# Where the outer sums of a nested Strassen-Winograd product are made: additions inside DMA transfers, another order of the outer products, and one addend taken with the PSUM read

## The chip, the cores and the metric

The kernel runs on one NeuronCore of a Trainium2 chip. The metric is device microseconds for one execution, as a median over runs. Five units matter here: TensorE (PE in the profile, with PEld for its weight loads), VectorE (DVE), ScalarE (ACT), GpSimd (POOL) and SyncE (SP), which here only issues DMA transfers. Each of them works through its own queue of instructions strictly in order; an instruction whose semaphore has not come holds everything behind it on that engine.

## The reference

What is computed, for x of 1024 x 512, 64 weight matrices (weight is 64 x 512 x 512, index e first), a linear weight of 512 x 512 and a bias, all in fp32:

```python
out_lin = x @ lin_w.T + lin_b
xv = jnp.einsum('bf,efm->bem', x, weight)
zp = jnp.einsum('bf,efm->bem', jnp.square(x), jnp.square(weight))
interaction = 0.5 * jnp.sum(jnp.square(xv) - zp, axis=1)
return out_lin + interaction
```

The second einsum needs no large product: the sum over e can be taken over the squared weight first, so it is one more product of 1024 x 512 by 512 x 512. The first one, x times a weight of 512 x 32768, is the work. Only the square of each element of xv is used, summed over e; the sign of a column of xv does not matter.

## The kernel before

**Tiling.** The 32768 columns (m and e together) are cut into 16 groups of 2048 columns. In a group the product (1024 x 512) by (512 x 2048) is done by Strassen-Winograd twice, one inside the other. The outer level cuts the group's weight into four quadrants w11, w12, w21, w22, each 256 x 1024 and 1 MB, held as two halves of 128 partitions x 1024 (`w11.0`, `w11.1` and so on), and replaces eight products by seven, numbered 1 to 7, of an x combination (`X1` to `X7`, made once at the start) with a weight combination. Products 1, 2, 3 use w11, w21, w22 as loaded; 5, 6, 7 and 4 use the outer sums T1 = w12 - w11, T2 = w22 - T1, T3 = w22 - w12 (written over w12) and T4 = w21 - T2 (written over w21; the sign that this form needs is in the x side). The order of the outer products is `ORDER = (1, 6, 2, 7, 4, 5, 3)`.

The inner level (`tree`, L393) does the same with each outer product: four sums t1 to t4 of 128 x 512 pieces of the weight combination, always on POOL, and then seven inner products, two matmuls of 128x128 by 128x512 each. That makes 7 x 7 x 2 = 98 matmuls a group and 1568 in all; 32 more for the linear part at the start and 32 for the squared weight at the end make 1632. An fp32 matmul is two PE records.

**From PSUM to the result.** The inner products go to three kinds of PSUM bank pair: b1, b3 and a ring of two b2. P5 goes to b3 first and is copied to an SBUF buffer p5 by ACT, then P3 is added in the same bank and the sum is copied to p53. P1 goes to b1 and is copied by ACT into the b2 pair that P6, P7 and P4 will add to. Each tree ends in four result positions (pos 0 to 3): for pos 0 and 2 DVE adds the PSUM bank to an addend in SBUF (`outer_psum`, L428), for pos 1 and 3 DVE adds p53 or p5 to the bank and a second addition of two SBUF buffers brings in the addend (`outer_sbuf`, L442). The addends are the running outer combinations `oa0..3` and `ob0..3`: which of the two an outer product reads is in ADDEND, which it writes in TARGET. Products 2, 4, 5 and 3 finish a quadrant of the result: `finish` squares it on ACT in place and reduces it over e on DVE into `acc`. `w_squares` (L371) squares each raw quadrant on ACT and reduces it on DVE into `w2_sum`.

**What sets the order.** Every operation is handed to `Plan.add` (L43) with its cost on each engine that may do it, its reads and writes. `Plan.order` (L62) gives each a latest time by working back from the chain of matmuls, whose order is fixed by a key (7 times the tree's number plus PLACE), and then simulates the engines: each takes the ready operation with the earliest latest time. An addition of two SBUF buffers has a cost on DVE and on POOL (`two_input`, L244) and goes to whichever takes it first, DVE only when it is due within `spare`; a sum that reads PSUM is DVE's only. The program is then written out in that order, so a wrong cost in the planner means a wrong order in a queue, not a race.

With PLACE the PE order around tree s is: P1 of s, P5 of s+1, P4 of s-1, P6 and P2 of s, P3 of s+1, P7 of s. So three inner products lie between P5 and P3 of a tree, which share bank b3.

**Loads and outer sums.** `load` (L355) fetches the four quadrants as eight transfers of 512 KB on SP's queue. `outer_sum` (L361) makes T1, T2, T3 and T4, two halves each, as additions that only DVE may do (`whole`, L256, with `only=DVE`). T1 and T2 are single buffers, and so are w11, w12 and w21; only w22 has two (w22a, w22b). The loop that calls all this is at L475.

```python
def whole(o, a, b, sub=False, only=None, psum=False):
    costs, emit = two_input(buf[o], buf[a], buf[b], sub, psum=psum)
    plan.add({e: c for e, c in costs.items() if only in (None, e)}, emit, (a, b), (o,))
```

Of the kernel before, what the change touches and what calls it, by code (L numbers as in the profile page):

```python
# [13 lines left out]
ALU = mybir.AluOpType  # L14
AX = mybir.AxisListType

P = 128
G = 2
ORDER = (1, 6, 2, 7, 4, 5, 3)

# [6 lines left out]
class Plan:  # L27
# [7 lines left out]

    HOP = 0.12

# [4 lines left out]

    def add(self, costs, emit, reads=(), writes=(), key=None, land=0.0):  # L43
        op = SimpleNamespace(
            n=len(self.ops), costs=costs, emit=emit, key=key, land=land,
            deps=set(), succ=[], latest=None, ready=0.0, end=None,
        )
        for r in reads:
            if r in self.writer:
                op.deps.add(self.writer[r])  # L50
        for w in writes:
            op.deps.update(self.readers[w])
            if w in self.writer:
                op.deps.add(self.writer[w])
        for r in reads:
            self.readers[r].append(op.n)
        for w in writes:
            self.writer[w], self.readers[w] = op.n, []
        op.deps.discard(op.n)
        self.ops.append(op)  # L60

    def order(self, spare=6.0):  # L62
        ops = self.ops
# [24 lines left out]
        free = dict.fromkeys(pending, 0.0)  # L88
        times = [0.0]
        done, late, nxt = [], 0.0, 0  # L90

        def release(o):
            for e in o.costs:
                pending[e].add(o.n)

        for o in ops:
# [3 lines left out]
        def pick(e, now):  # L100
            if e == PE:
                if nxt < len(chain):
                    o = chain[nxt]
                    if not left[o.n] and o.ready <= now:
                        return o
                return None
            for n in sorted((n for n in pending[e] if ops[n].ready <= now),
                            key=lambda n: (ops[n].latest, n)):
                o = ops[n]
                if len(o.costs) > 1 and e == DVE and o.latest + late - now > spare:  # L110
                    continue
                until = now + o.costs[e]
                if not any(
                    now < ops[u].ready < until - 0.2
                    and ops[u].latest < o.latest
                    and ops[u].latest + late < until + 0.1
                    for u in pending[e]
                ):
                    return o
            return None  # L120

        while len(done) < len(ops):
            now = heapq.heappop(times)
            moved = True
            while moved:
                moved = False
                for e in pending:
                    if free[e] > now:
                        continue
                    o = pick(e, now)  # L130
                    if o is None:
                        continue
                    moved = True
                    if e == PE:
                        nxt += 1
                        late = max(late, now - o.latest)
                    free[e] = now + o.costs[e]
                    heapq.heappush(times, free[e])
                    o.end = free[e] + o.land
                    for f in o.costs:  # L140
                        pending[f].discard(o.n)
                    done.append((o, e))
                    for x in o.succ:
                        left[x] -= 1
                        ops[x].ready = max(ops[x].ready, o.end + self.HOP)
                        if not left[x]:
                            release(ops[x])
                            heapq.heappush(times, ops[x].ready)
        return done
# [3 lines left out]
def kernel(  # L153
# [6 lines left out]
    out: bass.AP,  # L160
):


# [58 lines left out]
    for q in ("w11", "w12", "w21", "w22a", "w22b", "T1", "T2"):  # L222
        for c in range(NCB):
            make(f"{q}.{c}", half)
    for pos in range(4):
# [18 lines left out]
    def two_input(o, a, b, sub, size=1024, psum=False):  # L244

        costs = {DVE: 0.15 + 1.09 * size / 1024}
        if not psum:
            costs[POOL] = 0.2 + 2.25 * size / 1024

# [6 lines left out]
    def whole(o, a, b, sub=False, only=None, psum=False):  # L256

        costs, emit = two_input(buf[o], buf[a], buf[b], sub, psum=psum)
        plan.add({e: c for e, c in costs.items() if only in (None, e)}, emit, (a, b), (o,))

# [9 lines left out]
    def reduce(o, i, reads, writes):  # L270
        plan.add(
            {DVE: 1.22},
            lambda _: nc.vector.tensor_reduce(  # L273
# [58 lines left out]
    for i, n in ((1, "A11"), (2, "A12"), (4, "A22")):  # L332
        act(block4(i), a_ap(n), None, a_parts(n), (f"X{i}",))
    for i, a, b, sub in ((5, "A21", "A22", 0), (6, "X5", "A11", 1), (7, "A11", "A21", 1), (3, "A12", "X6", 1)):
        costs, emit = two_input(block4(i), a_ap(a), a_ap(b), sub)
        plan.add(costs, emit, a_parts(a, b), (f"X{i}",))
    for i in ORDER:
        x = buf[f"X{i}"]
        a11, a21, a12, a22 = (x[:, s, :] for s in range(4))
        s1, s2, s4 = (x[:, s, :] for s in range(4, 7))  # L340
        for o, a, b, sub in ((s1, a21, a22, 0), (s2, s1, a11, 1), (s4, a12, s2, 1), (a21, a11, a21, 1)):
            costs, emit = two_input(o, a, b, sub, 256)
            plan.add(costs, emit, (f"X{i}",), (f"X{i}",))
    for n in a_buf.values():
# [9 lines left out]

    def load(g):  # L355
        for q in (0, 1, 3, 2):
            for c in range(NCB):
                n = f"{w(g, QUAD[q])}.{c}"
                dma(buf[n], weight[g, q][:, c], (), (n,))

    def outer_sum(g, which):  # L361
        o, a, b = {
            1: ("T1", "w12", "w11"),
            2: ("T2", w(g, "w22"), "T1"),
            3: ("w12", w(g, "w22"), "w12"),
            4: ("w21", "w21", "T2"),
        }[which]
        for c in range(NCB):
            whole(f"{o}.{c}", f"{a}.{c}", f"{b}.{c}", True, DVE)

    def w_squares(g, q):  # L371
        row, col = divmod(QUAD.index(q), 2)
        for c in range(NCB):
            n, sq = f"{w(g, q)}.{c}", wsq_ring()
            act(buf[sq], buf[n], AF.Square, (n,), (sq,), 1.07)
            m = g * MG + (2 * col + c) * MI
# [10 lines left out]
    ADDEND = {6: "oa", 2: "oa", 7: "ob", 4: "oa", 3: "ob"}  # L387
    TARGET = {1: "oa", 6: "ob", 2: "oa", 7: "oa", 3: "ob"}
    RHS = {1: "w11", 2: "w21", 3: "w22", 4: "w21", 5: "T1", 6: "T2", 7: "w12"}
# [3 lines left out]
    def tree(s, g, i):  # L393
        r = [f"{w(g, RHS[i])}.{c}" for c in range(NCB)]
        b11, b21, b12, b22 = (buf[r[c]][:, k, :] for c in range(NCB) for k in range(KH))
        t = {k: t_ring[k]() for k in range(1, 5)}
        for k, a, b, reads in (
            (1, b12, b11, (r[0], r[1])),
            (2, b22, buf[t[1]], (r[1], t[1])),
            (3, b22, b12, (r[1],)),  # L400
            (4, b21, buf[t[2]], (r[0], t[2])),
        ):
            costs, emit = two_input(buf[t[k]], a, b, True, 512)
            plan.add({POOL: costs[POOL]}, emit, reads, (t[k],))
        rhs = {
            1: (b11, r[0]), 2: (b21, r[0]), 3: (b22, r[1]), 4: (buf[t[4]], t[4]),
            5: (buf[t[1]], t[1]), 6: (buf[t[2]], t[2]), 7: (buf[t[3]], t[3]),
# [17 lines left out]
        def target(pos):  # L425
            return f"{TARGET[i]}{pos}" if i in TARGET else c_ring()

        def outer_psum(b, pos):  # L428
# [3 lines left out]
            elif i == 5:  # L432
                for n in (f"oa{pos}", f"ob{pos}"):
                    whole(n, n, b, psum=True)
                finish(g, i, f"oa{pos}", pos)
            else:
# [5 lines left out]
        def outer_sbuf(b, p, pos):  # L442

            if i == 1:
                whole(f"oa{pos}", b, p, psum=True)
            elif i == 5:
                whole(p, b, p, psum=True)
                for n in (f"oa{pos}", f"ob{pos}"):
                    whole(n, n, p)
                finish(g, i, f"oa{pos}", pos)  # L450
            else:
                a, o = f"{ADDEND[i]}{pos}", target(pos)
                z = p if o == a else o
                whole(z, b, p, psum=True)
                whole(o, z, a)
                if i in (2, 4, 3):
# [3 lines left out]
        product(5, "b3", True)  # L460
        copy(p5, "b3")
        product(3, "b3", False)
# [12 lines left out]
    for g in range(NG):  # L475
        acc_name[g] = acc_ring()
        load(g)
        outer_sum(g, 1)
        outer_sum(g, 2)
        w_squares(g, "w12")  # L480
# [16 lines left out]

    xe = {(h, q): (f"w11.{q}", f"w12.{q}")[h] for h in range(2) for q in range(2)}
    last = acc_name[NG - 1]
    edge = M - MG  # L500
    acc_all = ("T2.0", "T2.1", w(NG, "w22") + ".0", w(NG, "w22") + ".1")
    lin_all = ("w21.0", "w21.1", "T1.0", "T1.1")
    for (h, q), n in xe.items():
# [87 lines left out]
```

## Time and profile before

The time is 1483.96 us, median of 3 runs (1482.59 to 1484.35). The profiled execution spans 1483.1 us, with TensorE's clock granted in full.

| engine | busy us | share of the span | instructions |
|---|---|---|---|
| PE (matmul) | 1427.1 | 96% | 3264 |
| DVE | 1265.6 | 85% | 1004 |
| POOL | 1178.8 | 79% | 693 |
| ACT | 748.2 | 50% | 756 |

The DMA engines move 83.5 MB, 56 GB/s over the span. How to read it: PE's busy time counts a matmul up to its modelled end, so 96% does not mean that 96% of the time is needed; what PE needs is found from the distance of its starts where nothing holds it up. A group of instructions is given by line, engine and operation; L252 is the line at which a helper issues every addition, so the groups have to be told apart by the names of their tiles (`oa`, `ob`, `p`, `c`, `t`, `T1.0`). The chain of waits follows the end back through what released each step: where it stays on PE, PE sets the time; where it changes to another engine, PE was waiting for that one, directly or by a buffer.

### The profile page before, as it was taken

Reading aid. Unit: us, or ns where it says so; the run is one execution under the profiler, and the core shown is the slowest. Engines: PE = TensorE matmul, PEld = TensorE weight load, DVE = VectorE, ACT = ScalarE, POOL = GpSimd, SP = SyncE. Lnnn points to the kernel's source line nnn. Section 1 sums busy time; section 2 is a strip of 40 time slices with the busy share of each in tenths; the row PEclk is TensorE's granted clock in tenths of the full one; section 3 lists DMA queues with packets and bytes.
Section 4 is the critical chain, followed back from the end, with each engine's and each line's share of the span. In section 5 each row is a group of like instructions: output and inputs, shape, how many; then the busy total and the mean of one; then the engine's idle time right before and its main releaser. Section 6 shows DMA issues by size and latency. Waiting matters only on the chain.

```text
span 1483.1 us, 10769 instructions
## 1 busy us (share of the span) xinstructions
PE 1427.1 (96%) x3264; PEld 613.4 (41%) x3264; DVE 1265.6 (85%) x1004; ACT 748.2 (50%) x756; POOL 1178.8 (79%) x693
## 2 busy tenths in 40 slices
PE   7999999999999999999999999999999999999998
PEld 3443434444343443434444343444434344343443
DVE  2699797988979799797988979799797979979894
ACT  2465554545445465555556555454554546555441
POOL 6987886878878688886878888687897878888781
PEclk9999999999999999999999999999999999999999
DMA  5312111111111121111111111111111111210221
GB/s 205 114 57 61 43 57 32 57 46 57 57 45 46 32 65 51 51 49 32 57 47 57 57 47 57 32 57 47 57 48 40 45 46 57 60 43 29 85 71 57
DMA packets 40376, 83.53 MB, mean 56 GB/s; under 512 B 18240, under 2 KB 19264, under 8 KB 40320
## 3 DMA queue, kind: packets, MB, share of 16 engines
q1 hardware_dynamic: 39664, 81.54, 17.4%
q10 hardware_dynamic: 576, 1.05, 0.2%
q8 instruction: 27, 0.44, 0.1%
q14 instruction: 29, 0.24, 0.1%
q0 software_dynamic: 80, 0.26, 0.0%
HBM read 76.68 MB, written 6.16 MB: 56 GB/s over the span
## 4 chain that ended last, share of the span: by engine, by line
PE 70%; DVE 24%; issue 5%; DMA 0%; ACT 0%; DVEq 0%; SPq 0%
PE b L415 66%; DVE ob L252 6%; DVE p L252 4%; DVE acc L273 3%; DVE T1.0_82 L252 3%; DVE oa L252 2%; PE b L302 2%; PE b L542 2%; DVE T1.1_83 L252 2%; DVE c L252 1%; DVE T2.0_84 L252 1%; DVE w_sum L273 1%; DVE w12.1_75 L252 1%; DMA ob<-lin_wT 0%; ACT p L264 0%
## 5 line engine op out<-in xcount | busy, mean ns | idle before, releaser
L415 PE MATMUL b<-t,X 128*128 128x512 f32 x1792 | 811.8, 594 | 17.2 <-DVE p L252 16.5
L415 PEld LDWEIGHTS b<-t,X 128*128 128x128 f32 x1792 | 336.5, 190 | 460.8 <-issue 433.0
L264 ACT COPY p<-b 128x1024 f32<-128x1024 f32 x224 | 225.6, 1007 | 306.0 <-PE b L415 177.3
L266 ACT ACTIVATE oa<-oa 128x1024 f32<-128x1024 f32 x128 | 133.6, 1055 | 119.3 <-DVE oa L252 93.1
L273 DVE TENSOR_REDUCE w_sum<-wsq 128x16 f32<-128x1024 f32 x128 | 154.9, 1212 | 31.8 <-ACT wsq L266 31.7
L264 ACT COPY b<-b 128x1024 f32<-128x1024 f32 x112 | 112.1, 1000 | 115.6 <-PE b L415 113.1
L273 DVE TENSOR_REDUCE acc<-oa 128x16 f32<-128x1024 f32 x128 | 154.3, 1206 | 4.5 <-ACT oa L266 4.5
L252 DVE TENSOR_TENSOR p<-b,p 128x1024 f32<-128x1024 f32 x96 | 116.3, 1211 | 10.9 <-PE b L415 10.9
L415 PE MATMUL b<-w21.0_76,X 128*128 128x512 f32 x256 | 120.3, 592 | 0.0
L252 POOL TENSOR_TENSOR oa<-oa,p 128x1024 f32<-128x1024 f32 x32 | 88.1, 2752 | 21.4 <-DVE p L252 19.3
L266 ACT ACTIVATE c<-c 128x1024 f32<-128x1024 f32 x64 | 66.1, 1056 | 69.3 <-DVE c L252 57.6
L252 POOL TENSOR_TENSOR c<-c,oa 128x1024 f32<-128x1024 f32 x32 | 75.4, 2355 | 31.6 <-DVE c L252 31.5
L252 POOL TENSOR_TENSOR oa<-p,oa 128x1024 f32<-128x1024 f32 x32 | 75.6, 2363 | 28.8 <-DVE p L252 28.8
L252 DVE TENSOR_TENSOR ob<-b,oa 128x1024 f32<-128x1024 f32 x32 | 39.0, 1220 | 62.8 <-PE b L415 62.8
L266 ACT ACTIVATE ob<-ob 128x1024 f32<-128x1024 f32 x64 | 67.6, 1058 | 43.8 <-DVE ob L252 35.5
L252 POOL TENSOR_TENSOR t<-w21.0_76,t 128x512 f32<-128x512 f32 x32 | 41.2, 1287 | 59.1 <-PE b L415 59.1
L252 POOL TENSOR_TENSOR oa<-oa,ob 128x1024 f32<-128x1024 f32 x32 | 76.6, 2393 | 4.2 <-DVE oa L252 4.2
L252 DVE TENSOR_TENSOR oa<-b,p 128x1024 f32<-128x1024 f32 x64 | 77.8, 1215 | 1.5 <-PE b L415 1.5
L273 DVE TENSOR_REDUCE acc<-c 128x16 f32<-128x1024 f32 x64 | 75.9, 1206 | 1.1 <-ACT c L266 1.1
L252 POOL TENSOR_TENSOR ob<-p,ob 128x1024 f32<-128x1024 f32 x32 | 75.6, 2361 | 0.9 <-DVE p L252 0.9
L252 POOL TENSOR_TENSOR ob<-ob,oa 128x1024 f32<-128x1024 f32 x32 | 75.3, 2352 | 0.8
L273 DVE TENSOR_REDUCE acc<-ob 128x16 f32<-128x1024 f32 x64 | 75.5, 1202 | 0.0
(127 smaller groups left out, 2343.8 us busy)
## 6 DMA issues: line engine op xcount, KB each, us to landing
w11.0_72<-weight SPq DMA_DIRECT2D x16, 512.0 KB, 3.7
w11.1_73<-weight SPq DMA_DIRECT2D x16, 512.0 KB, 4.6
w12.0_74<-weight SPq DMA_DIRECT2D x16, 512.0 KB, 3.8
w12.1_75<-weight SPq DMA_DIRECT2D x16, 512.0 KB, 3.7
w21.0_76<-weight SPq DMA_DIRECT2D x16, 512.0 KB, 3.8
w21.1_77<-weight SPq DMA_DIRECT2D x16, 512.0 KB, 4.7
w22a.0_78<-weight SPq DMA_DIRECT2D x8, 512.0 KB, 3.8
w22a.1_79<-weight SPq DMA_DIRECT2D x8, 512.0 KB, 3.8
```

What stands on the lines that cost most here:

```text
L252: f(o, a, b)
L264: nc.scalar.copy(o, i)
L266: nc.scalar.activation(o, i, func)
L273: lambda _: nc.vector.tensor_reduce(o, i.rearrange("p a (m e) -> p a m e", e=E), axis=AX.X, op=ALU.add),
L302: nc.tensor.matmul(buf[bank][:, j, :], buf[f"oa{2 * h + q}"][:, r, ts((g * G + j) % (NB // 2), P)], buf[f"ob{q}"][:, r, :], start=(k == 0) ...
L415: nc.tensor.matmul(buf[b][:, j, :], buf[f"X{i}"][:, SLOT[p], ts(j, P)], op, start=first, stop=True, skip_group_check=True,)
L542: nc.tensor.matmul(buf[bank][:, j, :], buf[xe[h, k // KH]][:, k % KH, ts((g * G + j) % (NB // 2), P)], w2_sum[:, k, :], start=(k == 0), st ...
```

## The change

Three things are altered, with the planner's constants adjusted beside them.

1. **Outer sums by accumulating DMAs.** T1 and T2 are no longer computed on DVE. A plain load puts w11 into the T1 and T2 buffers, and DMAs issued from POOL's queue with `accum_op=ALU.add` add w12 (for T1), or w12 and then w22 (for T2), straight from HBM. w12 gets w22 added from HBM in the same way once its squares are taken, and w21 gets T2 added from SBUF. The DMA form used here adds, so the signs are turned: T1 = w11 + w12, T2 = w11 + w12 + w22, T3 = w12 + w22, T4 = w21 + T2. The x combinations are turned to fit (X5 = A22 - A21, X6 = -X5 - A11, X3 = -X6 - A12); what is left over is the sign of whole columns of xv, which the square removes. The quadrants become buffers of 1 MB, loaded by one DMA each. The aim is to take the sums off DVE.
2. **Order of the outer products** 1, 6, 2, 7, 5, 4, 3: product 4, which needs w21 + T2, comes one later. As oa is still an addend for 4, product 5 writes its finished quadrant to a `c` buffer.
3. **P5 leaves PSUM with its addend.** In the trees of products 2, 7, 4 and 3 the ACT copy of P5 becomes a DVE addition of bank b3 and the addend of position 3; the later addition of two SBUF buffers for that position falls away.

In the planner, HOP, `spare` and the costs of DVE and POOL operations change, and it now lengthens the planned time of DVE and POOL additions that overlap. The diff, cut to its core:

```diff
-ORDER = (1, 6, 2, 7, 4, 5, 3)
+ORDER = (1, 6, 2, 7, 5, 4, 3)
...
-    HOP = 0.12
+    HOP = 0.18
...
-    def order(self, spare=6.0):
+    def order(self, spare=4.0):
...
-                    free[e] = now + o.costs[e]
+                    cost = o.costs[e]
+
+                    if e == DVE and o.both and free[POOL] > now + 0.1:
+                        over = free[POOL] - now
+                        cost += 0.9 * over
+                        longer(POOL, 0.35 * over)
+                    elif e == POOL and free[DVE] > now + 0.1 and running[DVE].both:
+                        over = free[DVE] - now
+                        cost += 0.5 * over
+                        longer(DVE, 0.9 * over)
+                    free[e] = now + cost
...
-        costs = {DVE: 0.15 + 1.09 * size / 1024}
+        costs = {DVE: 0.08 + 1.06 * size / 1024}
         if not psum:
-            costs[POOL] = 0.2 + 2.25 * size / 1024
+            costs[POOL] = 0.14 + 2.19 * size / 1024
 
...
-        plan.add({e: c for e, c in costs.items() if only in (None, e)}, emit, (a, b), (o,))
+        plan.add({e: c for e, c in costs.items() if only in (None, e)}, emit, (a, b), (o,),
+                 both=not psum)
...
         act(block4(i), a_ap(n), None, a_parts(n), (f"X{i}",))
-    for i, a, b, sub in ((5, "A21", "A22", 0), (6, "X5", "A11", 1), (7, "A11", "A21", 1), (3, "A12", "X6", 1)):
-        costs, emit = two_input(block4(i), a_ap(a), a_ap(b), sub)
-        plan.add(costs, emit, a_parts(a, b), (f"X{i}",))
+
+    def x_sum(i, o, a, b, kind, reads, size):
+
+        if kind != "-a - b":
+            costs, emit = two_input(o, a, b, kind == "a - b", size)
+        else:
+            costs = {DVE: two_input(o, a, b, True, size)[0][DVE]}
+
+            def emit(_):
+                nc.vector.scalar_tensor_tensor(o, a, -1.0, b, ALU.mult, ALU.subtract)
+
+        plan.add(costs, emit, reads, (f"X{i}",), both=True)
+
+    for i, a, b, kind in (
+        (5, "A22", "A21", "a - b"),
+        (6, "X5", "A11", "-a - b"),
+        (7, "A11", "A21", "a - b"),
+        (3, "X6", "A12", "-a - b"),
+    ):
+        x_sum(i, block4(i), a_ap(a), a_ap(b), kind, a_parts(a, b), 1024)
...
-    def load(g):
-        for q in (0, 1, 3, 2):
-            for c in range(NCB):
-                n = f"{w(g, QUAD[q])}.{c}"
-                dma(buf[n], weight[g, q][:, c], (), (n,))
+    def load(g, q):
+        n = w(g, QUAD[q])
+        dma(buf[n], weight[g, q], (), (n,), 4.8)
+
+    def load_more(n, src, reads=()):
+
+        plan.add(
+            {POOL: 1.0},
+            lambda _: nc.gpsimd.dma_start(buf[n], src, accum_op=ALU.add),
+            (n,) + reads, (n,), land=8.0,
+        )
 
     def outer_sum(g, which):
-        o, a, b = {
-            1: ("T1", "w12", "w11"),
-            2: ("T2", w(g, "w22"), "T1"),
-            3: ("w12", w(g, "w22"), "w12"),
-            4: ("w21", "w21", "T2"),
-        }[which]
-        for c in range(NCB):
-            whole(f"{o}.{c}", f"{a}.{c}", f"{b}.{c}", True, DVE)
+        if which < 3:
+            n = f"T{which}"
+            dma(buf[n], weight[g, 0], (), (n,), 4.8)
+            for q in (1, 3)[:which]:
+                load_more(n, weight[g, q])
+        elif which == 3:
+            load_more("w12", weight[g, 3])
+        else:
+            load_more("w21", buf["T2"], ("T2",))
 
...
         def target(pos):
-            return f"{TARGET[i]}{pos}" if i in TARGET else c_ring()
+            return f"{TARGET[i]}{pos}"
+
+        def early(pos):
+
+            return pos == 3 and i in (2, 7, 4, 3)
 
         def outer_psum(b, pos):
 
             if i == 1:
                 copy(f"oa{pos}", b)
             elif i == 5:
-                for n in (f"oa{pos}", f"ob{pos}"):
-                    whole(n, n, b, psum=True)
-                finish(g, i, f"oa{pos}", pos)
+                o = c_ring()
+                whole(o, f"oa{pos}", b, psum=True)
+                whole(f"ob{pos}", f"ob{pos}", b, psum=True)
+                finish(g, i, o, pos)
             else:
                 o = target(pos)
                 whole(o, b, f"{ADDEND[i]}{pos}", psum=True)
@@ -444,21 +506,28 @@
             if i == 1:
                 whole(f"oa{pos}", b, p, psum=True)
             elif i == 5:
+                o = c_ring()
                 whole(p, b, p, psum=True)
-                for n in (f"oa{pos}", f"ob{pos}"):
-                    whole(n, n, p)
-                finish(g, i, f"oa{pos}", pos)
+                whole(o, f"oa{pos}", p)
+                whole(f"ob{pos}", f"ob{pos}", p)
+                finish(g, i, o, pos)
             else:
                 a, o = f"{ADDEND[i]}{pos}", target(pos)
-                z = p if o == a else o
-                whole(z, b, p, psum=True)
-                whole(o, z, a)
+                if early(pos):
+                    whole(o, b, p, psum=True)
+                else:
+                    z = p if o == a else o
+                    whole(z, b, p, psum=True)
+                    whole(o, z, a)
                 if i in (2, 4, 3):
                     finish(g, i, o, pos)
 
         b2, p5, p53 = b2_ring(), p5_ring(), p53_ring()
         product(5, "b3", True)
-        copy(p5, "b3")
+        if early(3):
+            whole(p5, "b3", f"{ADDEND[i]}3", psum=True)
+        else:
+            copy(p5, "b3")
         product(3, "b3", False)
...
     for g in range(NG):
         acc_name[g] = acc_ring()
-        load(g)
+        load(g, 0)
+        outer_sum(g, 2)
+        for q in (1, 2, 3):
+            load(g, q)
         outer_sum(g, 1)
-        outer_sum(g, 2)
         w_squares(g, "w12")
         for idx, i in enumerate(ORDER):
```

## The prediction

> **What bounds the kernel now.** I read the page's busy times first, then the chain of waits, then the busy times by stage for one of the 16 weight groups.
>
> ```profile
> PE 1427.1 (96%) x3264; PEld 613.4 (41%) x3264; DVE 1265.6 (85%) x1004; ACT 748.2 (50%) x756; POOL 1178.8 (79%) x693
> ```
>
> Each matmul is two PE records. In undisturbed stretches of PE's timeline twelve records take 5.15 us from start to start (484.86 to 490.01), 0.429 us each, so 3264 records need 1400 us. Before the first matmul lie 8.4 us, after the last one 5.1 us. So with this arithmetic the span cannot go below about 1414 us; it is 1483, and 69 us are stalls of PE. The chain of waits shows where: one run of PE of about 58 us per group, and then a knot of VectorE.
>
> ```profile
> 483.04 58.31 PE b L415 x136
> 541.77 2.03 DVE T1.1_83 L252
> ...
> 557.50 2.53 DVE T1.0_82 L252
> 560.03 1.13 DVE p L252
> 561.16 1.13 DVE T2.0_84 L252
> 562.29 2.75 DVE ob L252
> ...
> 568.97 2.27 DVE ob L252 x2
> 571.29 68.95 PE b L415 x160
> ```
>
> Read it as the order in which the end is set: for 58 us nobody holds PE up, then for 30 us DVE does, in the stretch where a group's last product (3) meets the next group's first (1). The busy times by stage (length, then each engine) say the same:
>
> ```profile
> 483.04:571.29 88.25, 85.63 (x197) 36.74 (x197) 77.66 (x62) 46.48 (x48) 71.34 (x42) 1.00 0.16 49
> 483.04:541.50 58.46, 58.46 (x136) 25.94 (x137) 48.14 (x41) 30.73 (x31) 45.12 (x29) 1.00 0.14 44
> 541.50:571.29 29.79, 27.18 (x62) 10.80 (x60) 29.52 (x21) 15.75 (x17) 26.22 (x14) 1.00 0.19 58
> ```
>
> DVE (third figure) is 82% busy in the clean stretch and 99% in the knot. A group is 98 matmuls, 196 x 0.429 = 84.1 us; it takes 88.3 to 88.5 (483.04 to 571.29, 394.50 to 483.04). The stall is 4.2 to 4.4 us a group. From 41.74, where 3132 records of the groups are left, to 1450.40, where the last stage starts, are 1408.7 us; 3132 x 0.429 = 1343.8, so 65 us are stalls, 1.4 of them at the very end. The 15 knots hold about 63.5 us. The rest of the 69 is 4 us at the start.
>
> What fills the knot are outer sums, at more than the price of a clean addition:
>
> ```profile
> L252 DVE TENSOR_TENSOR T1.0_82<-w12.0_74,w11.0_72 128x1024 f32<-128x1024 f32 x16 | 40.6, 2537 | 18.3 <-DMA w12.0_74<-weight 18.3
> ...
> L252 POOL TENSOR_TENSOR t<-w11.1_73,t 128x512 f32<-128x512 f32 x16 | 35.0, 2189 | 0.0
> ...
> L252 POOL TENSOR_TENSOR t<-w11.0_72,t 128x512 f32<-128x512 f32 x16 | 20.6, 1289 | 0.0
> ...
> L252 DVE TENSOR_TENSOR T2.1_85<-w22b.1_81,T1.1_83 128x1024 f32<-128x1024 f32 x8 | 20.2, 2531 | 0.0
> ...
> L252 DVE TENSOR_TENSOR w12.0_74<-w22a.0_78,w12.0_74 128x1024 f32<-128x1024 f32 x8 | 9.7, 1207 | 0.0
> ```
>
> (busy us, mean ns, idle before.) An addition of the same shape takes 1.21 us or 2.53 us, and POOL's 128x512 one 1.28 or 2.2 us, where they lie on each other.
>
> **What the Trainium skill says.** *SBUF — State Buffer*, section "Who interferes with whom": a VectorE instruction with two SBUF inputs contends with a GpSimd one that reads SBUF, one input from PSUM does not. The trace agrees: the slow rows above are SBUF plus SBUF, and p<-b,p from PSUM stays at 1.21. *DMA: Bandwidth & Descriptors*, section "SWDGE vs HWDGE vs iDMA": an accumulating DMA can only be issued by GpSimd, whose cores write its descriptors; the trace has one DMA from POOL, the bias, 0.68 us busy. *Collectives: The Full Stack*, section "The bandwidth ceiling": an addition in the DMA engines costs two source reads, which halves the rate; no row of this trace shows it.
>
> **The change part by part, per group.**
>
> *Outer sums off DVE.* The twelve rows of T1, T2, w12 and w21 sums come to 242 us (40.6+32.4+32.3+21.0+20.2+19.5+18.3+18.3+10.7+9.7+9.7+9.7), 15.1 us a group for 8 instructions. In the knot shown, five of them hold DVE, start to next start, for 1.96+2.46+2.20+2.53+1.13 = 10.3 us. POOL gains too: four t rows at about 2.2 instead of 1.28 and two or three others, some 5 us a group.
>
> *P5 with its addend.* In products 2, 7, 4 and 3 one ACT copy (1.01 us, ACT is half idle) becomes a DVE addition from PSUM; DVE issues these every 1.13 us back to back, so +4.5 us a group. It takes away one SBUF addition each, 2.36 us on POOL, -9.4 us a group. The new wait: bank b3 is now freed by DVE, after the addend is there, and what is queued behind is P3 into the same bank, three products (5.1 us) after P5. For products 7 and 3 the addend ob3 is finished by two operations after the P7 two places before that P5 (1.2 on DVE, 2.4 on POOL); P5 and the three products take 8.6 us from that P7's end, so 3.8 us are spare. I cost it at 0.2 us a group; bounds 0 and 1.
>
> *DVE after.* 24 reductions, 24 additions for 6, 2, 7, 4, 3 with P5, 2 for product 1, 6 for 5: 56 x 1.13 = 63 us, with one contended SBUF addition 66, of 84.1. In the knot 29.5 - 10.3 + two P5 additions 2.3 = 21.5 us of work, for a PE time of 25.5 (29.8 - 4.3). It fits, so the 63.5 us go.
>
> *POOL after.* 28 t sums x 1.28 = 35.8, 10 SBUF additions x 2.36 = 23.6, five DMA issues at 0.7 (the bias row) to 2 us: 63 to 69 of 84.1, against 71.3 now. I take 1 us.
>
> *The accumulating DMAs.* T2 is a load of w11 plus two accumulations, T1 a load plus one, w12 and w21 one each: 6 plain and 5 accumulating transfers of 1 MB a group, for 4 plain MB now.
>
> ```profile
> q1 hardware_dynamic: 39664, 81.54, 17.4%
> ...
> w11.0_72<-weight SPq DMA_DIRECT2D x16, 512.0 KB, 3.7
> w11.1_73<-weight SPq DMA_DIRECT2D x16, 512.0 KB, 4.6
> ```
>
> 17.4% of 1483 us for 81.5 MB is 3.2 us per MB, so a plain 1 MB load lands after some 3.8 + 1.6 = 5.4 us. Accumulation is not in the trace: with two reads it is 5.4 + 3.2 = 8.6 us, from below 5.4, from above three passes and a colliding load, 15. I take 8.6 (the planner's own figure in the diff is 9). DMA engines: 6 x 3.2 + 5 x 6.4 = 51 of 84 us, busy but not the bound. What waits for them: POOL, in order, holds everything behind an accumulation until the transfer before it has landed. The t sums are two deep and POOL already idles 150 us on PE for lack of free t buffers, so it runs ahead; a wait of 1 to 2 us is hidden. T2 is free from the w21 sum (under product 5) to the next group's product 6, three to four products or 36 to 48 us; its chain of 5.4 + 2 x 8.6 = 23 fits.
>
> *Order 5 before 4* gives the w21 accumulation two products (24 us) between its last raw use and product 4. It only moves work: the squares of C22 go into a c buffer because oa is still an addend. Cost 0.
>
> *Start.* T2 of the first group is now two chained accumulations: x, linear weight, w11 and T2 are 5 MB, landed at about 20 us (3 MB plus three half loads were landed at 18.3), then 2 x 8.6 beside 4 MB of other loads, so 38 to 46 us. PE wants its sum at 45.3, after product 1's own P1, less 1.6 for the POOL sum. Between 0 and 3 us lost; I take 1.
>
> Sum: 1484.0 - 63.5 + 16 x 0.2 + 1 = 1424.7, say 1424.
>
> **The rivals.**
> *Most of it, part given back (0.20).* Accumulations land late (12 to 15 us), POOL stands some 6 us at two of them per group, 12 of its 20 idle us in lumps, and PE loses about 2 us a group: 1424 + 32 = 1456. For it: in-order waits, collisions with plain loads. Against it: POOL's lead.
> *No difference (0.02).* Another wait fills the knot to the same 4.3 us: 1484. Against it: both engines lose work exactly there.
> *Slower (0.12).* Descriptor writing is dear. At 6 us an issue POOL has 59.4 + 30 = 89.4 us a group, above PE's 84.1, and becomes the bound: 1424 + 16 x 5.3 = 1509. For it: the only POOL DMA in the trace has 2 KB rows, these have 8 KB and two inputs. Against it: 0.68 us for that one. An accumulation at a fifth of the plain rate would do the same by the DMA engines: 5 x 16 + 19 = 99 us a group.
>
> **How the numbers follow.** Knot gone 0.66, at 1424, from the floor (1414) to 1435; part given back 0.20, up to 1475; same 0.02; slower 0.12. Faster is 0.86. The range 1414 to 1472 leaves out the slower case, no change, and a few hundredths at either side.
>
> **What would show it.** Right: DVE near 1100 us and POOL near 1050, PE's groups 84 to 85 us apart, the t rows all at 1.28, hardly any DVE knot in the chain. The wrong steps would be seen as: POOL idle before its DMA issues, released by a landing (late accumulation); DMA issues on POOL of more than 2 us (descriptors); DMA share near 90% (transfers); PE waiting for DVE p at P3 (the P5 edit); PE's first groups late (start).

## The result and the profile after

The changed kernel takes 1429.13 us (median of 4 runs, 1428.62 to 1429.29) beside 1484.15 us for the kernel before on the same chip: a ratio of 0.963, 95% interval 0.961 to 0.965, or 55 us less. The profiled execution spans 1427.5 us.

The engines' busy times, from the first part of the page of the changed kernel:

```profile
PE 1409.1 (99%) x3264; PEld 617.9 (43%) x3264; DVE 1115.5 (78%) x946; ACT 678.8 (48%) x692; POOL 1010.6 (71%) x703
```

DVE lost 150 us, POOL 168 us. The chain of waits of the changed kernel (start us, us, what; "issue" is time for which the profile shows no wait):

```profile
194.32 0.57 issue
194.89 1.22 DVE p L280
196.10 0.04 issue
196.15 82.68 PE b L472 x192
...
278.88 0.57 issue
279.45 1.22 DVE p L280
280.67 0.04 issue
280.71 82.68 PE b L472 x192
```

Of the 30 us knot of VectorE at each group's end one DVE addition is left. A group's first P3 of product 3 starts at 196.15 and the next at 280.71: 84.56 us a group instead of 88.3 to 88.5. The bare matmul time is 196 x 0.429 = 84.1, so a group now stalls for 0.46 us instead of 4.3. The whole group (length, then PE, PEld, DVE, ACT, POOL, clock, DMA share, GB/s):

```profile
196.15:280.71 84.56, 84.38 (x196) 37.05 (x196) 68.10 (x58) 42.12 (x43) 61.42 (x44) 1.00 0.54 139
```

The busy times by stage hold a surprise. The first line is the first 55 us of a group, the second the 30 us up to the P1 of the next group's product 1, the place of the old knot:

```profile
211.70:266.45 54.75, 54.75 (x129) 24.32 (x128) 38.75 (x34) 24.80 (x26) 35.38 (x26) 1.00 0.38 107
266.45:296.27 29.82, 29.64 (x70) 12.73 (x69) 29.36 (x24) 17.32 (x18) 26.06 (x17) 1.00 0.85 198
```

The place of the old knot is as full of DVE as ever: 29.36 of 29.82 us, with 24 instructions instead of 21. But 70 PE records fit beside them now, where 62 did before (29.79 us), so PE hardly waits for them. Where the sums went shows in the groups of instructions (count, then busy us, mean ns, idle us before):

```profile
L280 DVE TENSOR_TENSOR c<-oa,p 128x1024 f32<-128x1024 f32 x15 | 53.7, 3581 | 0.0
...
L413 POOL DMA_DIRECT2D T<-weight x48 | 41.1, 856 | 5.2 <-DMA T<-weight 5.2
...
L413 POOL DMA_DIRECT2D w<-T x16 | 13.8, 864 | 0.0
L413 POOL DMA_DIRECT2D w<-weight x16 | 13.7, 856 | 0.0
```

and in the DMA queues and issues (KB each, median us to landing):

```profile
q0 software_dynamic: 11600, 84.15, 30.2%
q1 hardware_dynamic: 35056, 115.09, 23.3%
...
w<-weight SPq DMA_DIRECT2D x48, 1024.0 KB, 4.9
T<-weight POOLq DMA_DIRECT2D x48, 1024.0 KB, 8.2
T<-weight SPq DMA_DIRECT2D x32, 1024.0 KB, 4.8
w<-weight POOLq DMA_DIRECT2D x16, 1024.0 KB, 10.8
w<-T POOLq DMA_DIRECT2D x16, 1024.0 KB, 6.9
```

An accumulation occupies POOL for 0.86 us and lands after 7 to 11 us. The three T and w rows of POOLq are its kinds: onto w11 in T1 and T2, onto w12, and T2 onto w21. Together their packets take 30% of the time of the 16 DMA engines.

So far this reads like the prediction come true. The experiments say otherwise about what did it.

### The profile page after: what moved, and what is told of

The parts are those of the page before. It is cut to its first block, busy times and chain, and to the rows that moved or that the text cites. A ratio compares the mean times of both kernels' runs of the same rounds, so it can differ in the third digit from the quotient of the medians.

```text
span 1427.5 us, 10368 instructions
## 1 busy us (share of the span) xinstructions
PE 1409.1 (99%) x3264; PEld 617.9 (43%) x3264; DVE 1115.5 (78%) x946; ACT 678.8 (48%) x692; POOL 1010.6 (71%) x703
## 3 DMA queue, kind: packets, MB, share of 16 engines
q0 software_dynamic: 11600, 84.15, 30.2%
## 4 chain that ended last, share of the span: by engine, by line
PE 92%; DMA 2%; POOL 2%; DVE 2%; issue 1%; ACT 0%; DVEq 0%; SPq 0%; ACTq 0%; POOLq 0%
PE b L472 90%; DMA T<-weight 2%; PE b L617 2%; DVE p L280 1%; POOL t L280 1%; POOL X L280 1%; DMA oa<-xT 0%; POOL ob L280 0%; DVE ob L280 0%; ACT X L293 0%; SPq L309 0%; POOL w L413 0%; DVE w22a L280 0%; DVEq L662 0%; ACTq L309 0%
## 5 line engine op out<-in xcount | busy, mean ns | idle before, releaser
L472 PE MATMUL b<-w,X 128*128 128x512 f32 x768 | 358.5, 592 | 3.4 <-DVE p L280 2.3
L280 POOL TENSOR_TENSOR t<-w 128x512 f32<-128x512 f32 x128 | 163.2, 1278 | 147.5 <-PE b L472 84.5
L472 PEld LDWEIGHTS b<-w,X 128*128 128x128 f32 x768 | 145.7, 190 | 187.8 <-issue 175.1
L280 POOL TENSOR_TENSOR t<-w,t 128x512 f32<-128x512 f32 x128 | 164.9, 1289 | 57.5 <-PE b L472 57.3
L472 PE MATMUL b<-T,X 128*128 128x512 f32 x384 | 180.4, 592 | 0.0
L295 ACT ACTIVATE wsq<-w 128x1024 f32<-128x1024 f32 x96 | 98.0, 1054 | 70.0 <-DVE w_sum L302 66.5
L280 POOL TENSOR_TENSOR t<-T 128x512 f32<-128x512 f32 x64 | 83.5, 1305 | 47.5 <-issue 33.2
L472 PEld LDWEIGHTS b<-T,X 128*128 128x128 f32 x384 | 73.0, 190 | 91.8 <-issue 88.2
L280 DVE TENSOR_TENSOR oa<-b,oa 128x1024 f32<-128x1024 f32 x64 | 77.8, 1216 | 29.8 <-PE b L472 29.8
L280 POOL TENSOR_TENSOR t<-T,t 128x512 f32<-128x512 f32 x64 | 82.0, 1281 | 25.5 <-PE b L472 25.5
## 6 DMA issues: line engine op xcount, KB each, us to landing
w<-weight POOLq DMA_DIRECT2D x16, 1024.0 KB, 10.8
```

The lines of the kernel that those rows point to most:

```text
L280: f(o, a, b)
L295: nc.scalar.activation(o, i, func)
L472: nc.tensor.matmul(buf[b][:, j, :], buf[f"X{i}"][:, SLOT[p], ts(j, P)], op, start=first, stop=True, skip_group_check=True,)
```

## The experiments

**Theory A** is the prediction's: the gain is the 15 us of sums a group that leave DVE. **Rival B**: the new order of the outer products and the recalibrated planner made it. **Rival C**: it is the SBUF additions that the P5 part takes off POOL.

### Both parts crossed: sums on DVE or by DMA, P5 copied or added

The sums go back to DVE by one function (and loads in the order w11, w12, w22, w21 ahead of it):

```diff
-            for q in (1, 3)[:which]:
-                load_more(n, weight[g, q])
...
+        for c in range(NCB):
+            costs, emit = two_input(buf[o][:, c], buf[a][:, c], buf[b][:, c], False)
+            plan.add({DVE: costs[DVE]}, emit, (a, b), (o,), both=True)
```

P5 goes back to ACT by one line:

```diff
-            return pos == 3 and i in (2, 7, 4, 3)
+            return False
```

Sums on DVE, P5 added:

> The changed kernel with only the DMA part undone: T1, T2, w12 and w21 sums are again eight DVE additions a group, all else (order, P5 with its addend, planner) as changed. Theory A (the gain is the 15 us of outer sums a group that leave DVE): DVE rises from 68 to 81 to 84 us of a group's 84.1, the knot returns, 1475 to 1500 us. Rival B (order and the newly calibrated planner made the gain): at most 1445. Rival C (fewer SBUF additions on POOL made it): at most 1450.

Sums by DMA, P5 copied:

> The changed kernel with only the P5 part undone: P5 is copied by ACT in every tree and the addend comes by a second addition of two SBUF buffers. Theory A: DVE falls by 4.5 us a group, POOL rises by 9.4 from 61.4 to 71 of 84.1, no wait for ob3 before P3, so within 6 us of the changed kernel, 1423 to 1436. Rival C: most of the gain is lost, 1455 to 1480.

Sums on DVE, P5 copied, so that the new order and the new planner stay (and, with them, the 1 MB buffers and the turned signs):

> Both parts undone, with the new order of the outer products and the new planner kept: what these two are worth alone. Theory A: both are worth little, 1470 to 1490. Rival B: near the changed kernel, at most 1445. Together with the two runs before, it also gives what the P5 part is worth where the sums are on DVE: Theory A says it costs time there, since it adds 4.5 us a group to DVE, so this one is faster than the run with only the DMA part undone by 5 to 30 us.

Measured (us, and the ratio to the kernel before with its interval):

| | P5 added on DVE | P5 copied by ACT |
|---|---|---|
| sums by DMA | 1429.13, 0.963 (0.961 to 0.965), the changed kernel | 1426.38, 0.961 (0.959 to 0.962) |
| sums on DVE | 1434.32, 0.966 (0.965 to 0.968) | 1427.29, 0.962 (0.960 to 0.963) |

Theory A falls, and so does C. With all eight sums of a group back on DVE and P5 copied as before, the kernel is as fast as the changed one. The DMA part is worth 5.2 us where P5 is added on DVE and 0.9, within the intervals, where it is copied. The P5 part costs 7.0 us beside sums on DVE (clear by the intervals) and 2.8 beside sums by DMA (the intervals overlap). Neither of the two parts named first is needed for the gain. The four runs of the kernel with DMA sums and copied P5 spread from 1422.44 to 1427.54, so its small differences are the least sure. The busy times by stage of the run with both undone, in the same two stages of a group:

```profile
211.70:266.00 54.30, 54.30 (x128) 24.13 (x127) 48.67 (x41) 30.23 (x32) 43.25 (x28) 1.00 0.14 49
266.00:295.80 29.80, 29.80 (x70) 13.11 (x69) 25.60 (x22) 15.75 (x17) 28.56 (x15) 1.00 0.17 57
```

PE has no gap: 29.80 of 29.80. DVE has 74.3 us of work in a group of 84.1, where it had 77.7 before, and the last 30 us ask for 25.6 of it instead of 29.5. Two things lie behind this: other work stands in that place, and the same additions take less time, because they overlap less with POOL additions. The first two lines are from the kernel before, the others from the run with both undone:

```profile
547.11 2.53 DVE L252 TENSOR_TENSOR T2.1_85<-w22a.1_79,T1.1_83 128x1024 f32<-128x1024 f32 x1
L252 DVE TENSOR_TENSOR ob<-ob,p 128x1024 f32<-128x1024 f32 x15 | 50.4, 3363 | 0.0
...
L280 DVE TENSOR_TENSOR w<-w,T 128x1024 f32<-128x1024 f32 x32 | 71.2, 2224 | 0.0
L280 DVE TENSOR_TENSOR T<-w,w 128x1024 f32<-128x1024 f32 x32 | 45.7, 1427 | 18.8 <-DMA w<-weight 18.8
...
L280 DVE TENSOR_TENSOR ob<-ob,p 128x1024 f32<-128x1024 f32 x15 | 18.1, 1208 | 0.0
```

In the knot of before, six additions of two SBUF buffers take 14.0 us on DVE (2.03, 2.53, 2.28, 2.61, 1.21 and 3.36); in the same place of this run five take 7.5. Over the whole kernel such additions of 128x1024 take 293 us for 143 before and 240 for 144 here; alone, at 1.21 us, they would take 173 and 174. The difference is the 3.4 us a group by which DVE has less to do. How much of the gain is the shorter overlaps and how much the other place of the work, no run separates. The total alone doesn't decide: with sums on DVE and P5 added they take least, 197 us for 144, and that kernel is 7 us slower.

### The sums left out of the kernel before

```diff
...
-        for c in range(NCB):
-            whole(f"{o}.{c}", f"{a}.{c}", f"{b}.{c}", True, DVE)
+        if which < 3:
+            for c in range(NCB):
+                n = f"T{which}.{c}"
+                dma(buf[n], weight[g, 0][:, c], (), (n,))
```

> The kernel before with its outer sums left out: T1 and T2 are loaded with w11, w12 and w21 stay as loaded; order, P5 and planner of before. What taking the sums off DVE is worth without anything in their place and without the rest of the change. Theory A: the knot goes, groups 84.1 to 84.6 us apart, 1416 to 1430. Rivals B and C: 1455 or more, since order, planner and POOL's additions are as before.

Measured: 1420.94 us, ratio 0.957 (0.956 to 0.959). A group of it:

```profile
112.50:196.62 84.12, 84.12 (x198) 37.24 (x197) 62.22 (x54) 46.35 (x48) 66.80 (x42) 1.00 0.24 77
```

So the prediction's central step holds as far as it goes: without the sums the knot is gone, at 62 us of DVE a group, in the old order and with the old planner. Taking them away is enough. It is not needed, as the table above shows. What the DMA sums would do in the kernel before with its own order and planner was not run.

### Order alone, planner alone

> The kernel before, written out by the changed planner (hop, spare, costs, lengthening of additions of DVE and POOL that overlap); old order, sums on DVE, P5 copied. The run with both large parts undone left the new order and the new planner, and was as fast as the changed kernel: this splits the two. Theory P (the planner now knows what an overlapped sum costs, and puts the sums where DVE has room): 1424 to 1440. Theory O (the order of the outer products frees the knot): 1470 to 1490.

> The changed kernel with sums on DVE and P5 copied by ACT, written out by the planner of before: of the change only the order 1, 6, 2, 7, 5, 4, 3 is left (with 1 MB weight buffers and the turned signs). Theory O: 1424 to 1440, the stretch between a group's last and the next group's first product is free of waits. Theory P: 1470 to 1495, with the knot of DVE at the end of a group as before.

The first puts the changed `Plan` and these constants into the kernel before; the second puts the old ones into the run with both parts undone.

```diff
-    HOP = 0.12
+    HOP = 0.18
...
-        costs = {DVE: 0.15 + 1.09 * size / 1024}
+        costs = {DVE: 0.08 + 1.06 * size / 1024}
```

Measured: planner alone 1438.37 us, 0.969 (0.968 to 0.971); order alone 1443.10 us, 0.972 (0.971 to 0.974). P was expected to leave O at 1470 or more, or the other way round; neither happened. Each alone brings over 40 us of the 57 that both bring together. The run with the order alone also has the 1 MB buffers and the turned signs, and nothing separates the order from these; nor was it tried which of the planner's constants, or its rule for overlaps, makes the gain of the planner. The same two stages of a group, planner alone:

```profile
211.89:267.28 55.39, 55.39 (x131) 24.53 (x130) 48.86 (x42) 31.18 (x32) 43.00 (x29) 1.00 0.17 50
267.28:297.10 29.82, 29.00 (x69) 12.62 (x68) 27.50 (x20) 15.38 (x16) 26.30 (x14) 1.00 0.18 54
```

and order alone:

```profile
214.69:270.38 55.69, 55.69 (x131) 24.69 (x130) 45.98 (x39) 30.02 (x31) 44.35 (x28) 1.00 0.14 49
270.38:300.20 29.82, 28.82 (x68) 12.38 (x67) 29.82 (x24) 16.36 (x17) 28.73 (x15) 1.00 0.18 58
```

The groups are 85.2 and 85.1 to 85.5 us long, stalls of 1.1 and of 1.0 to 1.4 us. With the order alone DVE is busy for all of the last 30 us and PE still loses only a quarter to a third of what it lost before. What is left in the planner's run is one thing, in its chain of waits:

```profile
287.63 0.60 POOL t L274
288.23 3.30 POOL oa L274
...
292.51 1.00 ACT p L287
293.51 0.04 issue
293.56 6.70 PE b L438 x15
```

A POOL addition of 2.36 us alone takes 3.30 beside a DVE sum of two SBUF buffers (T2.0, 3.36 us, from 289.23), ACT squares its result and only then copies p53, and P3 waits for that copy. The planner knows of such overlaps now, and in the old order it did not avoid this one.

The planner of before under the whole change:

> The changed kernel, written out by the planner of before: its waits (0.12 us a hop), its spare, its costs of DVE and POOL operations and no lengthening of overlapping additions. Theory A: the order in the queues is a little worse, 1426 to 1445. Rival B (the calibration made the gain): 1455 or more.

Measured: 1431.43 us, 0.964 (0.963 to 0.966), 2 us from the changed kernel. So beside the DMA sums the planner is worth little; beside sums on DVE it is worth 1443.1 - 1427.3 = 15.8. The gains do not add up: any one of three things, taking the sums away, the order (with its buffers), or the planner, breaks most of the knot, and the next finds little left.

### The old order under DMA sums

```diff
-ORDER = (1, 6, 2, 7, 5, 4, 3)
+ORDER = (1, 6, 2, 7, 4, 5, 3)
...
-            return pos == 3 and i in (2, 7, 4, 3)
+            return pos == 3 and i in (2, 7)
```

> The changed kernel with the old order 1, 6, 2, 7, 4, 5, 3; product 4 writes to c and 5 to oa as before. P5 takes its addend only in the trees of 2 and 7, because in the old order the addend of 4 and of 3 comes from the tree directly ahead, whose P7 lies behind their P3. Theory A: POOL +4.7, DVE -2.3 us a group, the w21 accumulation has 12 us instead of 24, so 1425 to 1445. If the order is itself worth time (late w21 sum): 1445 to 1480.

Measured: 1600.60 us, 1.078 (1.075 to 1.082), slower than the kernel before by 116 us and worse than both expectations. Its chain of waits through one group:

```profile
300.35 12.20 DMA w<-weight
...
312.63 1.06 ACT wsq L295
313.70 0.02 issue
313.72 0.04 DVE w_sum L302
...
320.65 44.91 PE b L472 x104
...
366.12 6.90 DMA w<-T
373.02 0.07 issue
373.09 1.27 POOL t L280
```

Twice a group in-order engines stand on a transfer. ACT waits for a quadrant to square until the load lands, 12.2 us after its issue; DVE stands 4.8 us on the reduction of that square, with additions that PE needs behind it. POOL issues the w21 sum when PE has last read the raw w21 (it waited 2.65 us for that); the next t sums, for product 4, cannot start until it lands after 6.9 us, and POOL, with one other addition to do, stands 3.7 of these. A group takes 95 us (302.25 to 397.27), in which DVE is busy 65 and POOL 66: neither is full, the time is latency. TensorE's granted clock averaged 0.976 in this run; the missing 2.4% of 1602 us are 38, too little for 116 us. The planner reckons with 6.3 us for such a load (4.8 of SP's time and 1.5 to land); why it takes 12.2 here was not tried.

With the new planner and the same 1 MB buffers, the order is thus what makes DMA sums possible. It also makes the P5 addition possible: in the old order, products 4 and 3 take their addend from the product directly ahead, whose P7 stands at key 7s - 1 while their own P3, at 7s - 2, waits for the bank that the addition frees. The expectation of this run says so; the prediction had not seen it.

### What an accumulation costs

Left out:

```diff
-        plan.add(
-            {POOL: 1.0},
-            lambda _: nc.gpsimd.dma_start(buf[n], src, accum_op=ALU.add),
-            (n,) + reads, (n,), land=8.0,
-        )
+        return
```

> The changed kernel without its 80 accumulating DMAs: T1 and T2 hold w11 alone, w12 and w21 stay as loaded, so those sums are left out. It shows what the accumulations still cost. Theory A (hidden in the steady state, 3 us lost at the start to a late landing): groups still 84.5 us apart, the stall near 70 us gone, 1423 to 1428. If POOL's issues and waits cost time in each group: below 1421.

As plain copies:

```diff
-            lambda _: nc.gpsimd.dma_start(buf[n], src, accum_op=ALU.add),
+            lambda _: nc.gpsimd.dma_start(buf[n], src),
```

> The changed kernel with the 80 accumulations turned into plain copies of the same 1 MB from the same queue, so T1, T2, w12 and w21 hold the last source alone. It prices accumulation apart from the issue by POOL. If an accumulation costs a second read: the copies of weight land 3 us earlier than the accumulations' 8.2, at about 5, and the queue's share of the DMA engines falls from 30% to about 15%. If the extra time is that of POOL's issue: they stay at 8.

Measured: without accumulations 1420.78 us, 0.957 (0.956 to 0.959), with copies in their place 1421.03 us in a single run. So 80 DMAs on POOL's queue cost nothing as such; it is the accumulation that costs some 8 us. The queues and issues of the run with copies:

```profile
q0 software_dynamic: 11600, 84.15, 16.3%
...
T<-weight POOLq DMA_DIRECT2D x48, 1024.0 KB, 5.1
...
w<-T POOLq DMA_DIRECT2D x16, 1024.0 KB, 4.6
```

The copy of 1 MB lands after 5.1 us, the accumulation after 8.2, and the queue's share of the DMA engines is 16.3% for the copies and 30.2% for the accumulations. The ratio, 30.2 / 16.3 = 1.85, fits what the Trainium skill says in *Collectives: The Full Stack*, section "The bandwidth ceiling", of the additions of a ReduceScatter: each needs two source reads, which halves the rate. The reads themselves are not seen in these traces. An issue also holds POOL longer:

```profile
L413 POOL DMA_DIRECT2D T<-weight x48: 553/562/564, 13.1 to 1293.3; - x48
```

(minimum, median and maximum ns, first and last start), 0.56 us against 0.86 in the changed kernel.

The 8 us come in two pieces. In the groups: the run with copies has the same instructions and the same P5 additions, and PE's step before P3 of product 3 is 275.97 - 274.19 = 1.78 us instead of 280.71 - 278.65 = 2.06. POOL's `ob` addition ahead of that P5 ends later by 0.28 us (3.81 us behind the start of the PE run at 273.50, 3.53 behind the same one of the copies), about what the issue before it takes longer, and DVE's sum beside it takes 3.58 us instead of 3.30. From the first `w22a` P3 of the third group to the last stall of PE the changed kernel needs 1112.7 us (280.71 to 1393.42), the run with copies 1109.2 (275.97 to 1385.19). The other 4 to 5 us lie in the start, where the changed kernel's chain reads:

```profile
46.73 15.47 DMA T<-weight
...
62.34 0.10 POOL t L280
...
70.94 2.31 POOL ob L280
...
73.27 0.06 DVE p L280
...
76.81 32.90 PE b L472 x76
```

The accumulation into T1, issued at 46.73 among the first group's loads, lands after 15.5 us instead of 8.2. POOL comes to a t sum for product 5, which PE does not need yet, and stands 4.6 us on it. Behind it is the `ob` addition; DVE, at the P5 addition of product 7, stands 8.3 us on that; PE loses 3.0 us.

### Two versions put together

```diff
-            return pos == 3 and i in (2, 7, 4, 3)
+            return pos == 3 and i in (2, 7, 4, 3) and g == NG - 1
```

> A version put together from the runs so far: new order and planner, accumulating DMAs except for T1 and T2 of the first group, which DVE adds (it is idle there), and P5 copied by ACT except in the last group, where its addition shortens the end. Expected from the stalls seen: no stall in the groups, some 4 us less at the start than the changed kernel and the 1.4 us at the end kept, 1419 to 1424. If the late landings move elsewhere: 1426 or more.

> The same without any accumulating DMA: new order and planner, all sums on DVE, P5 copied by ACT except in the last group. If the DMA part is worth nothing once order and planner are new: 1422 to 1427, no slower than the changed kernel. If DVE at 86% is too close to its limit: 1430 or more.

Measured: 1425.26 us, 0.961 (0.959 to 0.962), with T1 and T2 of the first group on DVE and all other sums by DMA, and 1423.78 us, 0.960 (0.958 to 0.961), with no sums by DMA. The first is 1 us above its expected stretch: PE waits twice at the start, 1.74 us for a t sum and 1.45 for the ACT copy behind it. The second has the lowest median of all kernels that leave nothing out, and its interval lies below that of the changed kernel. Its chain is one piece of PE from 48.81 to 1383.03; a window of it:

```profile
189.84 260.50 PE b L472 x607
```

## Why the prediction was right or wrong

The time was right: 1424 was forecast with a range of 1414 to 1472, and 1429.13 came. The place was right too: the stall of 4.3 us a group between product 3 and the next product 1 was what there was to gain, and it went. What made it go was only half seen, and that the sum came out is in part luck: the forecast counted the 63.5 us once, for the sums leaving DVE, and since the gains do not add, a single count is right whichever of the three is credited.

- **"It fits, so the 63.5 us go", put down to the outer sums leaving DVE.** This step failed as an account of the change. Leaving the sums out does free the knot (1420.94), but in the change they leave together with a new order and a new planner, and these two do it with the sums still on DVE (1427.29). The step took the knot for a matter of load, 21.5 us of DVE work left in 25.5 of PE time. After the change DVE works 29.36 of the 29.82 us there, filled with other work, and PE loses 0.46: how full DVE is in that place does not say how long PE waits. Nor did the step ask what else could shorten the 10.3 us of outer sums in the knot: 4.6 of them are overlaps with POOL, beyond 1.21 us each.
- **"Order 5 before 4 ... only moves work ... Cost 0."** This failed. Order alone, with the turned signs and the 1 MB buffers that came along, brings 40.5 us (1483.62 to 1443.10), and without it the kernel with DMA sums and the new planner takes 116 us more than the kernel before.
- **The planner, its constants and its rule for overlaps, had no step at all.** Alone they bring 45.3 us (1483.62 to 1438.37). What they hold was in sight: the lengthening of overlapping additions and the sums' 2.5 us where the planner of before reckoned with 1.24.
- **P5 with its addend, costed at 0.2 us a group, bounds 0 and 1.** The wait came where it was looked for, at P3 of product 3 for ob3, and took 0.46 us a group with PE's restart: 15 x 0.46 = 6.9 us instead of 3.2. But the path was another: DVE was not waiting for POOL at that spot. It was still in an SBUF sum of 3.58 us that had started just after ob3's addition began on POOL, and in one reduction behind it. On the whole the part costs 3 to 7 us; its 9.4 us less of POOL work brought no gain that shows.
- **The accumulating DMA.** 8.6 us to land were estimated, 8.2 measured from HBM into T, 6.9 from SBUF, 10.8 into w12. Its share of the DMA engines was put at 32 of 84 us a group; 30.2% of the span is 25 us. The issue was put at 1 us, and is 0.86. The median landings and the issue are within the bounds, the one landing of 15.5 us at the start is just above them, and the share is below the estimate; the two ends that would have made it slower, 6 us an issue and a fifth of the rate, did not occur.
- **DVE 66 and POOL 63 to 69 us a group.** Measured 68.1 and 61.4, in the group from 196.15 to 280.71.
- **The start, costed at 1 us.** It lost 3.0, by T1's late landing rather than T2's. Against that the first matmul came at 5.96 us instead of 8.37.
- **The rivals.** "Part given back" had its mechanism right, POOL standing in order on a landing. It shows once, at the start, and it rules the run in the old order, where it costs far more than the 32 us reckoned and ends on the slower side. None of the rivals had the gain coming from somewhere else than the named parts.

## What to carry to other kernels

A full engine in the stretch where another one stalls shows where the wait is, not that its load is the cause: before a load is bought off, try what it costs to put the same work elsewhere. A change that also alters the order or the constants of a scheduler has to be costed with these as parts of their own, and its parts crossed with each other, because gains from one knot do not add. A DMA that takes over a computation brings its landing time into every in-order queue that uses the result, so it needs the slack in the order first.

## What the runs showed of the hardware that was not expected

- An accumulating DMA issue holds POOL for 0.86 us and a plain one of the same shape for 0.56.
- The first matmul starts at 5.96 to 6.5 us in the five runs in which a 1 MB weight load is the fifth DMA on SP's queue, and at 7.8 to 8.4 us in the eight others and the kernel before; the bias, issued on POOL, lands after 5.6 to 6.0 us instead of 7.5 to 8.0. What makes all first loads land sooner was not tried.
- What overlaps with POOL cost DVE depends on the placing. The 128 outer sums take 242 us before, 250 with the order alone, 236 with the planner alone, 220 with both, and 177 with both and P5 added on DVE, against 128 x 1.21 = 155 without any overlap. The time does not follow this sum.
- Once, in the run with DMA sums and P5 copied, a DVE addition of two SBUF buffers takes 7.78 us (from 102.82) while POOL does four additions one after the other (103.20 to 109.50); PE loses 3.2 us to it.
